# Selective scans on Trainium2: the backward scan written into the PSUM banks of the direction sum, and two fixed pairs of banks

## The chip, the cores and the metric

The kernel runs on one core of one Trainium2 chip. The metric is device time in microseconds, from three runs of the kernel before: 4045.58, 4043.1 and 4032.89 us, median 4043.1. One further execution was profiled.

The engines are named as in the profile: PE is TensorE (PEld its weight loads), DVE is VectorE, ACT is ScalarE, POOL is GpSimd, SP is SyncE. PSUM is the memory into which TensorE writes its sums. [...]

## The reference, cut to what matters

The network has two layers: attention with a mixture of experts, then a state-space layer with another mixture of experts. The change concerns the state-space layer alone. It runs one selective scan in four directions over an image of 32 x 32 positions and averages the four:

```python
def _selective_scan(x, A_log, D, W_delta, b_delta, W_B, W_C):
    delta = jax.nn.softplus(x @ W_delta + b_delta)
    Bm = x @ W_B
    Cm = x @ W_C
    A = -jnp.exp(A_log)
    dA = jnp.exp(delta[..., None] * A)
    dBx = (delta * x)[..., None] * Bm[:, :, None, :]
    ...
    _, h = jax.lax.associative_scan(combine, (dA, dBx), axis=1)
    y = jnp.einsum('blcn,bln->blc', h, Cm) + x * D
    return y
...
out1 = corr(flat)
out2 = jnp.flip(corr(jnp.flip(flat, axis=1)), axis=1)
rows_f = jnp.flip(rows, axis=1).reshape(B, H * W, C)
out3 = jnp.flip(corr(rows_f).reshape(B, H, W, C), axis=1).reshape(B, H * W, C)
cols_f = jnp.flip(cols, axis=1).reshape(B, W * H, C)
out4 = jnp.flip(corr(cols_f).reshape(B, W, H, C), axis=1)
...
mamba_out = (out1 + out2 + out3 + out4) / 4
```

Four images, 256 channels, 16 states and 1024 positions. The state obeys h = dA * h_before + dBx along the direction.

## The kernel before

**Stages.** The attention and the first mixture of experts fill the first 2191 us of the profiled execution, the scans the time from 2191 to 3461, and the second mixture of experts with the output the rest.

**What a scan is.** Channels lie on the 128 partitions, in two channel tiles, positions along the free dimension (1024). A `Scan` is one image, one channel tile and one state: 4 x 2 x 16 = 128 scans, in that order, worked one per *turn*. `turn(k)` gives out the instructions of scan k and of its neighbours in a pipeline, and `tc.manual_schedule()` keeps each engine's instructions in the order in which the code gives them out. So a turn has a fixed order on every engine, and an instruction that waits holds up what stands behind it on its engine.

**The four directions** of scan k become these instructions:

- `decays` (L2025, ScalarE): the decays along rows, into the PSUM tile `da`; a second set along columns (`column_decays`, L2017) and the products of decays along one row (`products`, L2021) lie in SBUF. `inputs` (L2033 GpSimd, L2034 ScalarE) makes the inputs `uu`, in row order and in column order.
- `forth` (L2046, VectorE): the forward scan, into the SBUF tile `h0`. TensorE adds it with the weight `twice` (two times the identity), since two of the four directions start from it.
- `back` (L2055, VectorE): the backward scan over the same decays, read in reverse, into an SBUF tile `h`. TensorE adds it with `ident`.
- `columns` (L2072, VectorE): the scan along columns, into another `h`; TensorE adds it transposed back (L2076).
- `come_in` and `third` (L2061 VectorE, L2066 GpSimd): the direction with flipped rows is the forward state plus a correction, products times a value that comes in for each row. TensorE adds the correction with `ident`.

**The sum.** `add` (L2041) multiplies a view of 1024 states by a weight in two halves of 512, one PSUM bank each, into the two tiles `hp` of the scan. Each of these fp32 matmuls shows as two instructions in the profile, so a direction is a *group* of four. The first group opens the accumulation (`start=True`). `output` (L2082, VectorE) multiplies each half of the sum by C into `yc`, and TensorE adds `yc` over the 16 states into the tile `y` (L2083); after the 16th state `finish` (L2088) adds y to the image. A turn thus has five groups on TensorE: columns and third of scan k-1, forward and backward of scan k, y of scan k-1.

**PSUM in this stage.** [...] The pool of four banks is shared with other steps, which ask it for a bank whenever they need one.

**Other steps in the turns.** At two places of a turn, at its top and after `come_in`, the kernel runs one piece of some other work: `norm` and `route` of the image before (the second mixture of experts' normalisation and routing), `Prep.steps` of the image after (its layer norm, delta, B and C), and `completing`, which fetches and adds results of the first mixture of experts. A piece after `come_in` typically issues TensorE's matmuls, and the piece at the top of the next turn reads them. VectorE reads the means (`nm_mean` L1690, `ln_mean` L1788), the variances (`ln_var` L1800), `ln_rb` (L1819), `raw` (L1703), `sums` (L1631) and `op` (L1911). ScalarE reads `bp` (L1828), `zp` twice (L1851, L1852) and `nm_tp` three times (L1704, L1707). About half of the 128 turns carry such matmuls. TensorE's order in a turn is: columns of k-1, third of k-1, forward and backward of k, y of k-1, then a step's matmuls.

GpSimd has also one indirect DMA in many turns: the routed tokens go out to their slots (L1983), or results are fetched (L1892). SyncE loads B and C of a scan two turns ahead (L2011, L2013).

Of the kernel before, what the change touches and what calls it, by code (L numbers as in the profile page):

```python
# [11 lines left out]
F32 = mybir.dt.float32  # L12
F16 = mybir.dt.float16
BF16 = mybir.dt.bfloat16
# [3 lines left out]
ALU = mybir.AluOpType  # L18
AX = mybir.AxisListType
PSUM = bass.MemoryType.PSUM  # L20

P = 128
# [3 lines left out]
HW = 32  # L26
L = HW * HW
NT = L // P
NTA = B * NT
HALF = 512  # L30
NHALF = L // HALF
# [31 lines left out]
def metaformer(ctx: ExitStack, tc: tile.TileContext, t: dict, out: bass.AP):  # L63
    nc = tc.nc

    cons = ctx.enter_context(tc.tile_pool(name="cons", bufs=1))
    ident = cons.tile([P, P], F32, tag="ident", name="ident")
# [3 lines left out]
    first = cons.tile([P, E], F32, tag="first", name="first")  # L71
# [398 lines left out]
    with ExitStack() as st:  # L470
        wp = st.enter_context(tc.tile_pool(name="a_w", bufs=1))
# [38 lines left out]
        p2 = st.enter_context(tc.tile_pool(name="a_p2", bufs=2))  # L510
# [403 lines left out]
        order = [(b, g, a, n) for b in range(B) for g in range(2) for a in range(NP) for n in range(2)]  # L914
# [13 lines left out]
        for b in range(B):  # L928
            i = b * PER
# [578 lines left out]
    with tc.If(some > 0):  # L1508
# [240 lines left out]
    twice = sw.tile([P, P], F32, tag="twice", name="twice")  # L1749
# [6 lines left out]
    h0s = [sw.tile([P, HW + 2, HW], F32, tag=f"h0_{i}", name=f"h0_{i}") for i in range(2)]  # L1756
    prods = [sw.tile([P, HW + 1, HW], F32, tag=f"prod{i}", name=f"prod{i}") for i in range(2)]
# [4 lines left out]
    def cols_flipped(a):  # L1762
        return a.rearrange("p (r w) -> p w r", w=HW)[:, ::-1, :]

    def grid(a):
        return a.rearrange("p (r w) -> p r w", w=HW)

    class Prep:
# [7 lines left out]
        def steps(self, room, psum, tag):  # L1776
# [62 lines left out]
            def lost(c, cols):  # L1839
                back = self.dx[:, c, cols]  # L1840
                nc.vector.tensor_scalar(back, v[:, c, cols], 1.0, 1.0, ALU.add, ALU.subtract)
                nc.vector.tensor_tensor(back, v[:, c, cols], back, ALU.subtract)
# [146 lines left out]
    with ExitStack() as st:  # L1989
        wp = st.enter_context(tc.tile_pool(name="s_w", bufs=1))  # L1990
        p1 = st.enter_context(tc.tile_pool(name="s_p1", bufs=1))
        p2 = st.enter_context(tc.tile_pool(name="s_p2", bufs=2))
        ps_m = ps_h = st.enter_context(tc.tile_pool(name="s_ps_h", bufs=4, space=PSUM))
        ps_y = st.enter_context(tc.tile_pool(name="s_ps_y", bufs=1, space=PSUM))
        ps_d = st.enter_context(tc.tile_pool(name="s_ps_d", bufs=1, space=PSUM))

        class Scan:

# [2 lines left out]

            def __init__(self, prep, k, c, s):
                self.prep, self.b, self.k, self.c, self.s = prep, prep.b, k, c, s
                self.h0, self.prod = h0s[k % 2], prods[k % 2]
                self.decay = am[:, c, s : s + 1]

            def rows(self):
# [25 lines left out]
                nc.gpsimd.tensor_tensor(self.uu[:, 0], self.prep.dx[:, self.c], self.bb, ALU.mult)  # L2033
                nc.scalar.copy(grid(self.uu[:, 1]), cols_flipped(self.uu[:, 0]))  # L2034

            def add(self, view, eye=None, first=False, last=False):

                if first:
                    self.hp = [ps_h.tile([P, HALF], F32, tag="hp", name="hp") for h in range(NHALF)]
                for h in range(NHALF):  # L2040
                    nc.tensor.matmul(self.hp[h], ident if eye is None else eye, view[:, ts(h, HW // NHALF), :],  # L2041
                                     start=first, stop=last)

            def forth(self):
                rows = self.h0[:, 1 : HW + 1, :]
                nc.vector.tensor_tensor_scan(rows.rearrange("p r w -> p (r w)"), self.da, self.uu[:, 0], 0.0,  # L2046
                                             ALU.mult, ALU.add)
                self.add(rows, eye=twice, first=True)

                self.gap = p2.tile([P, HW], F32, tag="gap", name="gap")  # L2050
                nc.gpsimd.tensor_tensor(self.gap, self.h0[:, 2:, HW - 1], self.h0[:, :HW, HW - 1], ALU.subtract)

            def back(self):
                hs = p2.tile([P, L], F32, tag="h", name="h", bufs=3)
                nc.vector.tensor_tensor_scan(hs[:, ::-1], self.da[:, ::-1], self.uu[:, 0][:, ::-1], 0.0,  # L2055
                                             ALU.mult, ALU.add)
                self.add(grid(hs))

            def come_in(self):
                self.come = p2.tile([P, HW], F32, tag="come", name="come")  # L2060
# [7 lines left out]
                self.add(grid(self.da_c), last=True)  # L2068

            def columns(self):  # L2070
                hs = p2.tile([P, L], F32, tag="h", name="h", bufs=3)
                nc.vector.tensor_tensor_scan(hs, self.da_c, self.uu[:, 1], 0.0, ALU.mult, ALU.add)  # L2072

                half = HW // NHALF
                for h in range(NHALF):
                    nc.tensor.matmul(cols_flipped(self.hp[h]), ident, grid(hs)[:, :, ts(h, half)],  # L2076
                                     start=False, stop=False)

            def output(self, y):
                for h in range(NHALF):  # L2080
                    yc = p2.tile([P, HALF], F32, tag="yc", name="yc", bufs=4)
                    nc.vector.tensor_tensor(yc, self.hp[h], self.cb[:, ts(h, HALF)], ALU.mult)  # L2082
                    nc.tensor.matmul(y[:, ts(h, HALF)], ident, yc, start=(self.s == 0), stop=(self.s == NS - 1))  # L2083

            def finish(self, y):
# [4 lines left out]
        order = [(b, c, s) for b in range(B) for c in range(CT) for s in range(NS)]  # L2090
        scans, steps, ys, cum = [], [], [], None
# [16 lines left out]
        def routed(b):  # L2108
            nonlocal sending
            yield from norm(b, tok, p1, ps_m, "hp", "hp", p1.tile([P, CT, L], F32, tag="xm", name="nm_d"))  # L2110
            yield from route(b, tok, slot, p1.tile([P, NUMBERS], F32, tag="numbers", name="numbers"), ps_m, "hp")
            sending = scatter(b)

        def turn(k):
            nonlocal steps, cum
            if k > 1:
                scans[k - 2].finish(ys[k - 2])
            for step in steps:
                next(step, None)
            next(complete, None)  # L2120
            if 0 <= k + 2 < len(order):
                b, c, s = order[k + 2]
                scans.append(Scan(preps[b], k + 2, c, s))
                scans[k + 2].rows()
            if k == -1:
                scans[0].decays()
            if 0 <= k + 1 < len(order):
                scans[k + 1].column_decays()
            if k > 0:
                scans[k - 1].third()  # L2130
            if 0 <= k + 1 < len(order):
                scans[k + 1].products(cum)
            if 0 <= k < len(order):
                b, c, s = order[k]
                if c == 0 and s == 0:
                    for left in (*steps, sending):
                        assert next(left, "end") == "end"
                    steps = []
                    if b + 1 < B:
                        preps.append(Prep(b + 1))  # L2140
                if b > 0 and c * NS + s == 1:
                    steps.append(routed(b - 1))
                if b + 1 < B and c * NS + s == (BEHIND if b > 0 else 0):
                    steps.append(preps[b + 1].steps(room, ps_m, "hp"))
                ys.append(ps_y.tile([P, L], F32, tag="y", name="y") if s == 0 else ys[-1])
                scans[k].forth()
                scans[k].back()
            if 0 <= k + 1 < len(order):
                if k >= 0:
                    scans[k + 1].decays()  # L2150
                scans[k + 1].inputs()
            next(sending, None)
            if k == NS * CT:
                assert next(complete, "end") == "end"
            if k > 0:
                scans[k - 1].output(ys[k - 1])
            if 0 <= k < len(order):
                scans[k].come_in()
                for step in steps:
                    next(step, None)  # L2160
                next(complete, None)
            if 0 <= k + 2 < len(order) and order[k + 2][2] == 0:

                b, c, _ = order[k + 2]
                if k < 0:
                    cum = lead.cum
                    return
# [17 lines left out]
    with ExitStack() as st:  # L2185
# [71 lines left out]
        with ExitStack() as sa:  # L2257
# [3 lines left out]
            ps_h = sa.enter_context(tc.tile_pool(name="m1_ps_h", bufs=3, space=PSUM))  # L2261
# [132 lines left out]
```

## Time and profile before

| what | value |
|---|---|
| profiled execution, whole | 4047.44 us |
| its span, first to last instruction | 4045.4 us |
| median of the runs | 4043.1 us |
| TensorE busy over the span | 3522.2 us (87%) |
| VectorE busy | 3049.1 us (75%) |
| ScalarE busy | 2818.0 us (70%) |
| GpSimd busy | 1894.3 us (47%) |
| granted TensorE clock over the span | 0.881 |
| each of L2046, L2055, L2072 (scans of 128 x 1024, 127 of the 128) | 2272, 2264, 2274 ns |
| yc, L2082 (128 x 512, 256 times) | 678 ns |
| fp32 matmul of 128 x 512 (L2083) | 592 ns, modelled to its end |

How to read it: the table is over the whole execution, and its stages have different limits, so the busy shares of the scan stage have to be taken by themselves. A matmul's duration contains the drain at its end, which overlaps the next one; how fast a train of matmuls runs is seen from the distance between starts. In a timeline a line has the start, the length, the engine, the source line, the operation, the tiles written and read, the number of instructions merged, and in brackets the idle time of the engine before it with what ended that. In a table of waits a line has who waited for whom, then the sum in us, the number of times and the longest one.

### The profile page before, as it was taken

The numbers are of one execution on the slowest core, as the hardware profiler recorded it, in microseconds if no ns is written. First come the engines' busy times: TensorE is split into PE (matmuls) and PEld (weight loads), VectorE is DVE, ScalarE is ACT, GpSimd is POOL, SyncE is SP. The second block draws the span as 40 slices with busy tenths as digits, with TensorE's granted clock in tenths as the row PEclk, the third lists the DMA queues.
The fourth block names the chain that finished last, engine by engine and source line by source line (L and its number), as shares of the span: only waits on it lengthen the run. The fifth ranks groups of instructions, "written<-read, shape, count | busy, mean of one in ns | idle before, by whom it ended". The sixth has DMA issues, their size and how long they took to land. (4 is left out here: it accounts for less than half of the span.)

```text
span 4045.4 us, 50460 instructions
## 1 busy us (share of the span) xinstructions
PE 3522.2 (87%) x17586; PEld 1963.0 (49%) x17586; DVE 3049.1 (75%) x5439; ACT 2818.0 (70%) x3748; POOL 1894.3 (47%) x1643
## 2 busy tenths in 40 slices
PE   8378888888788878886687999999999999999996
PEld 5134444534354434433564434444444434788885
DVE  2689898988899898987666899899899899411112
ACT  2889999999999998994255666767767677322222
POOL 0145454575548564765453665445445446121111
PEclk8568787788778877788798999999999999999997
DMA  9300093000000000000573333333333334565555
GB/s 293 102 1 1 1 260 90 1 1 30 12 1 1 17 17 1 1 12 22 176 214 120 119 118 122 104 104 125 106 109 122 114 106 135 192 189 188 188 191 188
DMA packets 241818, 393.76 MB, mean 97 GB/s; under 512 B 31888, under 2 KB 182160, under 8 KB 241424
## 3 DMA queue, kind: packets, MB, share of 16 engines
q1 hardware_dynamic: 218016, 340.54, 27.2%
q0 software_dynamic: 19904, 48.48, 3.7%
q8 instruction: 142, 2.33, 0.2%
q10 hardware_dynamic: 3632, 1.40, 0.1%
q14 instruction: 124, 1.02, 0.1%
HBM read 280.41 MB, written 109.94 MB: 96 GB/s over the span
## 5 line engine op out<-in xcount | busy, mean ns | idle before, releaser
L823 POOL TENSOR_SCALAR dr<-s_n,last 128x1024 bf16<-128x1024 f32 x250 | 719.7, 2895 | 734.8 <-DVE state L851 377.2
L733 ACT ACTIVATE junk_a<-s_n,state 128x1024 int8<-128x1024 f32 x448 | 514.6, 1149 | 23.7 <-DVE state L857 7.3
L2066 POOL TENSOR_TENSOR da_c<-prod,come 128x1024 f32<-128x1024 f32 x128 | 248.8, 1944 | 434.6 <-DVE h L2072 383.8
L737 DVE TENSOR_SCALAR_CACHE_REDUCE junk_v<-s_n,state 128x1024 int8<-128x1024 f32 x320 | 408.7, 1277 | 8.8
L2242 ACT ACTIVATE hid<-hp,b 128x256 f32<-128x256 f32 x288 | 133.7, 474 | 355.7 <-PE hp L2240 355.5
L784 DVE SCALAR_TENSOR_TENSOR w<-s_n,win 128x1024 f32<-128x1024 f32 x256 | 350.4, 1369 | 5.3
L787 DVE MAX8 win<-w 128x8 f32<-128x1024 f32 x256 | 314.5, 1228 | 8.8
L891 ACT ACTIVATE ex<-sT 128x1024 f32<-128x1024 f32 x256 | 247.1, 1016 | 88.7 <-PE sT L883 88.7
L2033 POOL TENSOR_TENSOR uu<-dx,bb 128x1024 f32<-128x1024 f32 x127 | 302.9, 2385 | 1.5 <-DMA bb<-bc_d 1.4
L733 ACT ACTIVATE junk_a<-s_n,guess 128x1024 int8<-128x1024 f32 x256 | 294.3, 1149 | 7.2
L2072 DVE TENSOR_TENSOR_SCAN h<-da_c,uu 128x1024 f32<-128x1024 f32 x127 | 288.8, 2274 | 0.0
L2046 DVE TENSOR_TENSOR_SCAN h<-da,uu 128x1024 f32<-128x1024 f32 x127 | 288.5, 2272 | 0.0
L2055 DVE TENSOR_TENSOR_SCAN h<-da,uu 128x1024 f32<-128x1024 f32 x127 | 287.5, 2264 | 0.0
L901 PE MATMUL o_ps<-ex,vT 128*32 128x256 f32 x2048 | 239.0, 451 | 54.0 <-ACT ex L891 42.2
L2017 ACT ACTIVATE da_c<-delta,a_log 128x1024 f32<-128x1024 f32 x128 | 268.5, 2097 | 5.3 <-DMA rows_y<-ys 5.2
L2076 PE MATMUL hp<-h,ident 128*128 128x512 f32 x512 | 248.9, 609 | 21.8 <-DVE h L2072 21.6
L2240 PE MATMUL hp<-xe,w 128*128 128x256 f32 x1152 | 258.6, 381 | 6.6 <-DVE xe L2228 6.4
L2251 DVE TENSOR_TENSOR ys<-yp,b2e 128x512 f32<-128x512 f32 x36 | 24.9, 692 | 317.2 <-PE yp L2248 305.1
L2253 POOL DMA_INDIRECT results<-ys,to x72 | 69.9, 970 | 409.2 <-DVE ys L2251 185.2
L767 ACT COPY s_n<-sp 128x1024 f32<-128x1024 f32 x256 | 245.3, 1003 | 19.1 <-PE sp L759 11.5
L2248 PE MATMUL yp<-w2e,hid 128*128 128x256 f32 x1152 | 255.9, 379 | 0.0
L2034 ACT COPY uu<-uu 128x1024 f32<-128x1024 f32 x127 | 252.3, 1987 | 2.5 <-POOL uu L2033 2.5
(646 smaller groups left out, 7787.0 us busy)
## 6 DMA issues: line engine op xcount, KB each, us to landing
cb<-bc_d SPq DMA_DIRECT2D x128, 512.0 KB, 4.0
bb<-bc_d SPq DMA_DIRECT2D x127, 512.0 KB, 4.9
w<-in_w SPq DMA_DIRECT2D x36, 1024.0 KB, 5.0
w2e<-in_w SPq DMA_DIRECT2D x36, 1024.0 KB, 5.6
slots_x<-zeros SPq DMA_DIRECT2D x1, 33669.0 KB
slots_x<-zeros SPq DMA_DIRECT2D x1, 33282.0 KB
w<-in_w SPq DMA_DIRECT2D x72, 256.0 KB, 3.1
xs<-slots_x SPq DMA_DIRECT2D x36, 261.0 KB, 3.8
```

Of the source, the lines that this page charges most:

```text
L733: nc.scalar.activation(junk, self.row(r), AF.Sign, bias=thr, scale=-1.0, accum_out=u)
L737: nc.vector.tensor_scalar(junk, self.row(r), thr, None, ALU.is_lt, ALU.add, accum_out=u)
L784: nc.vector.scalar_tensor_tensor(w, self.row(r), self.win[:, r, 0:1], self.row(r), ALU.is_gt if r < LAST_DVE else ALU.is_ge, ALU.subtract, ...
L787: nc.vector.max(out=self.win[:, r, 1:], in_=w)
L823: ins = eng.tensor_scalar(dr, self.row(r), self.last[:, r : r + 1], None, ALU.is_lt)
L2017: nc.scalar.activation(grid(self.da_c), cols_flipped(self.prep.delta[:, self.c]), AF.Exp, scale=self.decay)
L2033: nc.gpsimd.tensor_tensor(self.uu[:, 0], self.prep.dx[:, self.c], self.bb, ALU.mult)
L2046: nc.vector.tensor_tensor_scan(rows.rearrange("p r w -> p (r w)"), self.da, self.uu[:, 0], 0.0, ALU.mult, ALU.add)
L2055: nc.vector.tensor_tensor_scan(hs[:, ::-1], self.da[:, ::-1], self.uu[:, 0][:, ::-1], 0.0, ALU.mult, ALU.add)
L2072: nc.vector.tensor_tensor_scan(hs, self.da_c, self.uu[:, 1], 0.0, ALU.mult, ALU.add)
L2240: nc.tensor.matmul(hp[:, f % 2], self.w1[:, c, ts(f, P)], self.xe[:, c], start=(c == 0), stop=(c == CT - 1))
L2248: nc.tensor.matmul(yp[:, a], self.hid[:, f, ts(a, P)], self.w2[:, f, :], start=(f == 0), stop=(f == NF - 1))
```

## The change

The backward scan is no longer written to SBUF and added by TensorE. VectorE writes it straight into the two PSUM banks in which the scan's directions are summed, and TensorE adds the others onto it. [...] So before the scan, `begin` writes zeros with two bf16 matmuls of 512 columns (`nought`, one per bank) that open the accumulation. The forward states are then added after the backward scan, in `back`.

The four rotating banks become two fixed tiles `sum0` and `sum1` of two banks each; scan k owns `sums[k % 2]`. Other steps no longer ask a pool: `Spare` gives them the two halves of the pair that is not scan k's, from the output of scan k-1 (`ps_m.open(k)` stands after `come_in`) until `begin` of scan k+1 in the next turn. `begin` stands after the step pieces at the turn's top, and the matmuls of the column direction, before given out with the scan at a turn's end, stand behind it. TensorE's order in a turn becomes: opening pair of k, columns of k-1, third of k-1, forward addition of k, y of k-1, a step's matmuls. The column states `h` have two buffers instead of three (one such tile per turn instead of two).

```diff
-        ps_m = ps_h = st.enter_context(tc.tile_pool(name="s_ps_h", bufs=4, space=PSUM))
+        ps_h = st.enter_context(tc.tile_pool(name="s_ps_h", bufs=1, space=PSUM))
...
+        sums = [ps_h.tile([P, L], F32, tag=f"sum{i}", name=f"sum{i}") for i in range(2)]
+        nought = wp.tile([P, P], BF16, tag="nought", name="nought")
+        nc.vector.memset(nought, 0.0)
+
+        class Spare:
+
+            def open(self, k):
+                self.left = [sums[(k + 1) % 2][:, ts(h, HALF)] for h in range(NHALF)]
+
+            def tile(self, shape, dt, tag, name):
+                part = self.left.pop(0)
+                return part.rearrange("p (i c) -> p i c", c=shape[2]) if len(shape) == 3 else part
+
+        ps_m = Spare()
...
-            def add(self, view, eye=None, first=False, last=False):
-
-                if first:
-                    self.hp = [ps_h.tile([P, HALF], F32, tag="hp", name="hp") for h in range(NHALF)]
+            def begin(self):
+
                 for h in range(NHALF):
-                    nc.tensor.matmul(self.hp[h], ident if eye is None else eye, view[:, ts(h, HW // NHALF), :],
-                                     start=first, stop=last)
+                    nc.tensor.matmul(self.sum[:, ts(h, HALF)], nought, nought[:, 0:1].to_broadcast([P, HALF]),
+                                     start=True, stop=False)
+
+            def add(self, view, eye=None, last=False):
+
+                for h in range(NHALF):
+                    nc.tensor.matmul(self.sum[:, ts(h, HALF)], ident if eye is None else eye,
+                                     view[:, ts(h, HW // NHALF), :], start=False, stop=last)
...
-                self.add(rows, eye=twice, first=True)
...
             def back(self):
-                hs = p2.tile([P, L], F32, tag="h", name="h", bufs=3)
-                nc.vector.tensor_tensor_scan(hs[:, ::-1], self.da[:, ::-1], self.uu[:, 0][:, ::-1], 0.0,
+                nc.vector.tensor_tensor_scan(self.sum[:, ::-1], self.da[:, ::-1], self.uu[:, 0][:, ::-1], 0.0,
                                              ALU.mult, ALU.add)
-                self.add(grid(hs))
+                self.add(self.h0[:, 1 : HW + 1, :], eye=twice)
...
             def columns(self):
-                hs = p2.tile([P, L], F32, tag="h", name="h", bufs=3)
-                nc.vector.tensor_tensor_scan(hs, self.da_c, self.uu[:, 1], 0.0, ALU.mult, ALU.add)
-
+                self.hs = p2.tile([P, L], F32, tag="h", name="h")
+                nc.vector.tensor_tensor_scan(self.hs, self.da_c, self.uu[:, 1], 0.0, ALU.mult, ALU.add)
+
+            def columns_added(self):
                 half = HW // NHALF
                 for h in range(NHALF):
-                    nc.tensor.matmul(cols_flipped(self.hp[h]), ident, grid(hs)[:, :, ts(h, half)],
+                    nc.tensor.matmul(cols_flipped(self.sum[:, ts(h, HALF)]), ident, grid(self.hs)[:, :, ts(h, half)],
                                      start=False, stop=False)
...
             next(complete, None)
+            if 0 <= k < len(order):
+                scans[k].begin()
+            if k > 0:
+                scans[k - 1].columns_added()
...
                 scans[k].come_in()
+                ps_m.open(k)
                 for step in steps:
```

In `output` the two halves of `self.sum` take the place of the two tiles `self.hp`.

More of the change, by code (lines that the diff above doesn't have):

```diff
@@ L2003, in __init__ @@
                 self.prep, self.b, self.k, self.c, self.s = prep, prep.b, k, c, s
-                self.h0, self.prod = h0s[k % 2], prods[k % 2]
+                self.h0, self.prod, self.sum = h0s[k % 2], prods[k % 2], sums[k % 2]
                 self.decay = am[:, c, s : s + 1]
@@ L2081, in output @@
                     yc = p2.tile([P, HALF], F32, tag="yc", name="yc", bufs=4)
-                    nc.vector.tensor_tensor(yc, self.hp[h], self.cb[:, ts(h, HALF)], ALU.mult)
+                    nc.vector.tensor_tensor(yc, self.sum[:, ts(h, HALF)], self.cb[:, ts(h, HALF)], ALU.mult)
                     nc.tensor.matmul(y[:, ts(h, HALF)], ident, yc, start=(self.s == 0), stop=(self.s == NS - 1))
```

## The prediction

> **What bounds the kernel now.** I read the busy time by stage first. The scan stage is the only one the diff touches, and two engines are nearly full in it: TensorE works 1227 of its 1270 us, VectorE 1147 (span start to end, length, then busy time and instructions per engine, granted clock, DMA).
>
> ```profile
> 2191.00:3461.00 1270.00, 1227.35 (x3013) 533.99 (x3014) 1147.36 (x1123) 874.67 (x681) 673.94 (x464) 0.99 0.36 115
> ```
>
> So a TensorE saving can give at most what VectorE idles there, 1270 - 1147 = 123 us. VectorE's waits say how much of that is TensorE's load and how much is plain latency:
>
> ```profile
> DVE yc L2082 <- PE hp L2041: 28.7, 63, 2.4
> DVE lg L1703 <- PE raw L1701: 20.8, 12, 1.8
> DVE x L2088 <- PE y L2083: 14.4, 8, 2.1
> DVE nm_d L1690 <- PE nm_mean L1687: 12.1, 6, 2.0
> DVE xm L1788 <- PE ln_mean L1785: 11.1, 6, 3.7
> ```
>
> Then the timeline, turn by turn, from one L2046 to the next. A turn without extra steps late in the stage:
>
> ```profile
> 3392.63 2.27 DVE L2046 TENSOR_TENSOR_SCAN h<-da,uu 128x1024 f32<-128x1024 f32 x1
> 3394.82 2.27 DVE L2055 TENSOR_TENSOR_SCAN h<-da,uu 128x1024 f32<-128x1024 f32 x1
> 3397.44 0.69 DVE L2082 TENSOR_TENSOR yc<-hp,cb 128x512 f32<-128x512 f32 x1 [0.36 <-PE hp L2041]
> ...
> 3394.66 1.88 PE L2076 MATMUL hp<-h,ident 128*128 128x512 f32 x4
> 3396.38 1.88 PE L2041 MATMUL hp<-da_c,ident 128*128 128x512 f32 x4
> 3398.10 1.88 PE L2041 MATMUL hp<-h,twice 128*128 128x512 f32 x4
> ```
>
> Scans start 2.18 us apart, groups of four matmuls 1.72 us apart. TensorE has five groups a turn, 5 x 1.72 = 8.58, which is this turn's length; VectorE alone needs 7.86 (the turn from 3334.00 to 3341.85 has no idle). Elsewhere extra steps (norms, routing, preparing the next batch) stretch VectorE to 9 to 12 us, or put a sixth group on TensorE (10.30).
>
> **The change, part by part.** Removed: one group a turn, the backward addition, 1.72 us of TensorE. Added: two bf16 matmuls of 512 columns. A bf16 matmul with 128 columns takes 0.057 us of a train (16 in 1.07 us; less the last one's own 0.22, 15 distances), so four times as many columns 0.23, the pair 0.46, and with a restart after a wait 0.5. The other bound is the fp32 spacing, 0.43 each, 0.96. I take 0.5, as bf16 is the nearer row:
>
> ```profile
> 219.80 1.07 PE L883 MATMUL sT<-drop,dr 128*128 128x128 bf16 x16
> ```
>
> A plain turn then needs 4 x 1.72 + 0.5 = 7.4 of TensorE: VectorE becomes the bound, at 7.86. The forward addition now waits for the backward scan, and that is covered: y ends 0.2 us into a turn, the opening pair 0.7, columns 2.4, third 4.15 (yc needs its second half at 4.97), the backward scan 4.45, and the addition starts at 4.6, when the backward one did. Without that cover it would cost up to 1.72.
>
> Moved: the column additions go behind the opening pair and behind the steps' readers. This is the new wait. The pair for scan k+1 uses the banks in which the steps of turn k left their sums, so it waits until VectorE or ScalarE has read these; behind it on TensorE stand columns, third and the next addition, and VectorE's backward scan waits for the pair itself; behind that scan stand yc, come and columns, and ScalarE's L2025, which reuses the decays' banks and had 1.15 us of idle to spare in plain turns. Before, the columns' group ran during that reading. Memset, DMA issues and the queues of SyncE and GpSimd have nothing moved past them (one memset, before the stage's first turn).
>
> Scan into PSUM: no row has it. Reading from PSUM costs nothing visible (L2046, from PSUM, 2272 ns; L2072, from SBUF, 2274), ScalarE writes PSUM in 1115 ns (L2025) and SBUF in 1146 (L2021). That bounds it at -0.03 us below; above, by the farthest row, a whole further pass at 1.225 us (L2088). I take 0, nearest to the first pair, since only the memory differs there. [...]
>
> By kind of turn:
> - Plain turns bound by TensorE (116 to 127 of 0 to 127, 8.58 each): 12 x (8.58 - 7.86) = 8.7; turns 23, 24, 30 (0.59, 0.67, 0.73): 2.0. Gain 10.7.
> - Turns in which VectorE waits for y at a channel tile's end (L2088). y is now there at 4.6 + 2 x 1.72 + 0.2 = 8.24 into a turn, VectorE arrives at 7.85: 0.4 idle instead of 2.15 (three times), 1.43, and 1.1 in turn 16. Gain 5.2 + 1.0 + 0.7 = 6.9.
> - Steps read by VectorE (means, variances, raw). Most of their idle stays: the path is backward scan, addition, y, step, read, and the addition has only changed its name. Turns 33, 34: 11.18 now and after. What goes is backlog: turn 1 (12.82 to 11.18), 25 (idle 3.1 to the 0.7 of turn 26), 40 and 72 (12.31 to 11.18), five with 0.4 to 1.0: 1.6 + 2.4 + 2.3 + 2.7 = 9.0.
> - Steps read by ScalarE lose. From the zp group's start to the end of ScalarE's second reading are 2715.23 - 2712.04 = 3.19; then 0.1, the pair 0.5, and four groups 6.88: 10.67 a turn against 10.30. With the two bp turns before them, in which the pair waits for one reading of 0.58 and holds the backward scan by 1.3 and 0 us, and 2.0 before the first zp turn, turns 47 to 53 come to 8.5 + 11.5 + 8.2 + 11.7 + 3 x 10.67 = 71.9 against 69.5: batch 1 loses 2.4, batch 2 (70.8 before) 1.1, batch 0, where results are added in the same turns, gains 1.0. The four nm_tp turns of three batches (ScalarE reads until 1.1 us into the next turn) lose 0.7 a batch. Loss 2.4 + 1.1 - 1.0 + 2.1 = 4.6.
>
> ```profile
> 2712.04 1.88 PE L1847 MATMUL zp<-xm,wd 128*128 128x512 f32 x4
> ...
> 2714.55 0.68 ACT L1852 ACTIVATE sp<-zp,bd 128x512 f32<-128x512 f32 x1
> ```
>
> - Turn 0: its backward scan stood 3.1 us for a DMA that reads the buffer it overwrites; in PSUM it need not, but column decays wait for the same DMA. [...]
> - Clock. TensorE idles more, in stretches of over 2 us in some ten turns of 10 to 12.5 us. Before, a window of 3.4 us that was busy 1.04 or 1.40 us was followed by one at half clock, one busy 1.68 was not:
>
> ```profile
> 2987.10:2990.50 3.40, 1.04 (x10) 0.85 (x8) 3.40 (x3) 1.48 (x1) 0.00 (x0) 1.00 0.52 192
> 2990.50:2993.90 3.40, 3.40 (x4) 1.49 (x5) 3.40 (x4) 1.15 (x1) 1.92 (x2) 0.51 0.00 0
> 3301.20:3304.60 3.40, 1.40 (x4) 0.68 (x4) 3.40 (x2) 0.09 (x1) 1.31 (x1) 1.00 0.13 53
> ...
> 2669.70:2673.10 3.40, 1.68 (x4) 0.68 (x4) 3.40 (x4) 0.00 (x0) 1.59 (x1) 1.00 0.05 19
> ```
>
> Half a clock over 3.4 us is 1.7 us of TensorE, of which the next turn's slack (about 0.5) hides part: 1.2. I take three more such windows that matter, a loss of 3. [...]
>
> Sum: 10.7 + 6.9 + 9.0 - 4.6 + 1 - 3 = 20 us. The end gains nothing more: the last yc waits for the last scatter's DMA (5.1 us idle), which moves with turn 127. The profiled execution took 4047.4 (span 4045.4 and 2 around it), so 4027; the shown runs' median, 4043.1, lies 4 below it, so 4023.
>
> **The rivals.**
> - The opening is dear (0.96 instead of 0.5). For: it follows a wait every time and switches weights. Against: the bf16 row. Some 24 turns (12 zp, 12 nm_tp) run around TensorE and pay 0.46: 11 less, 4034, no change that can be measured (within 0.3%, 12 us, which is about what runs of this kernel tell apart).
> - The clock. For: the half windows above, and VectorE will be the bound in most turns. Against: in plain turns TensorE stays 94% loaded. If each of the 65 turns that carry a step's matmuls were followed by a half window, 65 x 1.2 = 78 less 20: 4101. It decides from 17 such turns (20 / 1.2); 27 of them give 4055, slower.
> - The scan into PSUM is slower. For: it would read and write PSUM at once, which no row shows. Against: a scan takes 2.1 ns an element, and ScalarE writes 1024 of them into PSUM in 1115 ns, half of that. It cancels the gain from 20 / 128 = 0.16 us a scan; at 0.25 the time is 4055, at the upper bound of 1.225 it is 4180.
> - The waits that I let go are latency too. For: most of VectorE's 115 us of waiting is the unchanged path above. Against: turns of the same kind without backlog (26, 33) are shorter. Without the 9.0 and 6.9 the gain is 4, the time 4039: no measurable change.
>
> **How the numbers follow.** Forecast 0.58: faster, 4006 to 4031. The dear opening 0.12 and waits that stay 0.10, together 0.22: 4032 to 4054. Clock 0.10, scan into PSUM 0.10: slower, from 4055. The best end: scan 4 faster, no clock loss (3), turn 0 (4), a low run (6): 4023 - 17 = 4006. The upper end takes in the whole second case and stops at 4054, where the slow cases begin, with 2 in 10 left out. Chances: faster by over 0.3% 0.58, within 0.22, slower 0.20.
>
> **What would show it.** In the changed profile: the backward additions (two groups' worth of x512) gone; pairs of bf16 matmuls of 0.2 us; turns 116 to 127 at 7.86; yc idle near 0; in zp turns the backward scan idle for the opening pair, turns of 10.7; L2055's successor still at 2.27 us; fewer than ten windows at half clock. I am wrong if that scan is over 2.4 us, if the pair takes nearly 1 us, or if backward scans wait in plain turns.

## The result, and the profile after

| | before | changed |
|---|---|---|
| median of 12 runs each, us | 4044.06 | 4048.23 |
| lowest to highest, us | 4032.89 to 4052.62 | 4032.59 to 4052.15 |
| ratio to before, 95% interval | | 1.000, 0.9985 to 1.0015 |
| profiled execution (its span), us | 4047.4 (4045.4) | 4032.7 (4030.7) |
| start of the first forward scan, us | 2191.29 | 2176.40 |
| scan stage: first to last forward scan, us | 1252.85 | 1252.85 |
| from the last forward scan to the end of the span, us | 601.3 | 601.5 |

The forecast was 20 us faster; nothing was gained. The two profiled spans differ by 14.7 us, but all of that lies ahead of the first forward scan (2191.29 - 2176.40 = 14.9), where the diff adds no more than one memset. So from here on kernels are compared by their scan stage, from the start of turn 0's forward scan to that of turn 127: 1252.85 us in both.

The stage in the changed kernel, busy time by engine (columns as in the prediction's window: PE, PEld, DVE, ACT, POOL, each with its instructions, granted clock, DMA share, GB/s):

```profile
2176.00:3446.00 1270.00, 1096.51 (x2758) 464.88 (x2757) 1147.66 (x1123) 874.90 (x681) 669.26 (x464) 0.98 0.36 115
```

TensorE lost 131 us of work (1227 to 1097). VectorE works as long as before (1147.4, now 1147.7) in as long a stretch. So its idle time, which was to shrink, is the same 122 us, and only its place has moved. VectorE's waits in that stretch:

```profile
DVE yc L2100 <- PE sum L2060: 46.7, 37, 2.8
DVE lg L1703 <- PE sum L1701: 13.6, 12, 1.5
DVE nm_d L1690 <- PE sum L1687: 12.1, 6, 2.0
DVE sum L2072 <- PE sum L2054: 11.5, 26, 1.3
```

The output product yc waits 46.7 us instead of 28.7, in 37 places instead of 63: the many small waits of the plain turns have gone and fewer, longer ones have come. The wait of the backward scan L2072 for the opening pair L2054 is new. Where the opening pair itself waits (TensorE's waits, same stretch):

```profile
PE sum L2054 <- ACT sum L1707: 22.8, 12, 1.9
PE sum L2054 <- ACT sp L1852: 13.5, 10, 1.4
PE sum L2054 <- DVE xm L1819: 13.0, 5, 3.5
PE sum L2054 <- DVE x L1911: 12.0, 8, 2.1
```

A plain turn, which starts at 3350.66 and ends at 3358.51 (timeline):

```profile
3350.66 2.27 DVE L2065 TENSOR_TENSOR_SCAN h<-da,uu 128x1024 f32<-128x1024 f32 x1
3350.84 0.60 PE L2054 MATMUL sum<-nought 128*128 128x512 bf16 x2
3351.28 1.88 PE L2094 MATMUL sum<-h,ident 128*128 128x512 f32 x4
3352.84 2.27 DVE L2072 TENSOR_TENSOR_SCAN sum<-da,uu 128x1024 f32<-128x1024 f32 x1
3352.99 1.88 PE L2060 MATMUL sum<-da_c,ident 128*128 128x512 f32 x4
3355.02 1.27 DVE L2100 TENSOR_TENSOR yc<-sum,cb 128x512 f32<-128x512 f32 x2
```

No line of VectorE has idle time in brackets, and the turn takes 7.86 us instead of 8.58. The opening pair costs 0.44 (3350.84 to 3351.28). So the first part of the forecast came true; the loss is elsewhere. Turn 37, one of the turns in which a norm's sums are read by ScalarE (nm_tp), before:

```profile
2566.83 1.96 PE L2076 MATMUL hp<-h,ident 128*128 128x512 f32 x4
2567.11 2.28 DVE L2046 TENSOR_TENSOR_SCAN h<-da,uu 128x1024 f32<-128x1024 f32 x1
...
2568.63 1.88 PE L2041 MATMUL hp<-da_c,ident 128*128 128x512 f32 x4
```

and in the changed kernel:

```profile
2551.05 0.17 DVE L1703 COPY lg<-sum 128x16 f32<-128x16 f32 x1 [1.01 <-PE sum L1701]
2551.14 2.28 DVE L2065 TENSOR_TENSOR_SCAN h<-da,uu 128x1024 f32<-128x1024 f32 x1
2551.26 0.59 ACT L1704 COPY tok<-sum 128x512 f32<-128x512 f32 x1 [2.82 <-DVE lg L1703]
...
2552.91 0.59 PE L2054 MATMUL sum<-nought 128*128 128x512 bf16 x2 [1.89 <-ACT sum L1707]
2553.34 1.88 PE L2094 MATMUL sum<-h,ident 128*128 128x512 f32 x4
2553.59 2.30 DVE L2072 TENSOR_TENSOR_SCAN sum<-da,uu 128x1024 f32<-128x1024 f32 x1 [0.17 <-PE sum L2054]
...
2555.05 1.88 PE L2060 MATMUL sum<-da_c,ident 128*128 128x512 f32 x4
...
2556.97 1.29 DVE L2100 TENSOR_TENSOR yc<-sum,cb 128x512 f32<-128x512 f32 x2 [1.08 <-PE sum L2060]
```

Before, the columns started 0.28 us ahead of the turn, beside ScalarE's reading, and the third group 1.52 us into it. Now the order is: ScalarE has read (1.71 into the turn), opening pair (1.77), columns (2.20), third (3.91), and yc at 5.83, 1.08 us after VectorE was free for it. The turn takes 10.54 us instead of 9.87.

Two differences stand in these lines, and either could be the cause. The **order**: columns and third stand behind the opening pair, and that behind the readers. The **whole pair as one tile**: ScalarE's tok waits for VectorE's lg, though they read different halves, and yc's first half starts after all four matmuls of the third group and not after its own two. A third difference is the **clock**: ten stretches at half clock (granted clock 0.5; each lasts 3.4 us, two of them 6.8) lie in the stage, against three before.

### The profile page after: what moved, and what is told of

Read it like the earlier page. It is cut to its first block, busy times and chain, and to the rows that moved or that the text cites. A ratio compares the mean times of both kernels' runs of the same rounds, so it can differ in the third digit from the quotient of the medians.

```text
span 4030.7 us, 49782 instructions
## 1 busy us (share of the span) xinstructions
PE 3380.4 (84%) x17330; PEld 1890.6 (47%) x17330; DVE 3050.2 (76%) x5440; ACT 2816.5 (70%) x3748; POOL 1887.5 (47%) x1643
## 5 line engine op out<-in xcount | busy, mean ns | idle before, releaser
L2083 POOL TENSOR_TENSOR da_c<-prod,come 128x1024 f32<-128x1024 f32 x128 | 247.0, 1930 | 466.3 <-DVE h L2089 442.2
L2072 DVE TENSOR_TENSOR_SCAN sum<-da,uu 128x1024 f32<-128x1024 f32 x127 | 289.3, 2278 | 11.5 <-PE sum L2054 11.5
L2065 DVE TENSOR_TENSOR_SCAN h<-da,uu 128x1024 f32<-128x1024 f32 x127 | 288.6, 2272 | 1.0 <-POOL uu L2048 1.0
L2094 PE MATMUL sum<-h,ident 128*128 128x512 f32 x512 | 256.9, 626 | 35.5 <-DVE h L2089 35.5
L2060 PE MATMUL sum<-h,twice 128*128 128x512 f32 x512 | 251.9, 615 | 41.4 <-DVE sum L2072 41.4
L767 ACT COPY s_n<-sp 128x1024 f32<-128x1024 f32 x256 | 245.4, 1003 | 25.4 <-PE sp L759 17.8
```

Of the source, the lines that this page charges most:

```text
L2072: nc.vector.tensor_tensor_scan(self.sum[:, ::-1], self.da[:, ::-1], self.uu[:, 0][:, ::-1], 0.0, ALU.mult, ALU.add)
```

## The experiments

Where no ratio is given, the scan stage of one profiled execution is what is compared. Half-clock stretches do not fall alike in two executions of one kernel: e5 and e8 below are the same kernel and have nearly the same stage, yet turns 1, 12 and 111 differ by 1.7, 1.7 and 2.5 us between them. So what a kernel does is read from the turns at full clock, and a few us of a stage mean little.

**e1: columns first.** The two calls in `turn` exchanged:

```diff
-            if 0 <= k < len(order):
-                scans[k].begin()
             if k > 0:
                 scans[k - 1].columns_added()
+            if 0 <= k < len(order):
+                scans[k].begin()
```

> One edit to the changed kernel: in each turn the column matmuls of the turn before are issued ahead of the opening pair instead of behind it. Measure: the scan stage, from the start of the first forward scan to the start of the last, 1252.85 us in the kernel before and in the changed one. Theory A (order: the opening pair stands behind the readers of the side steps, the column matmuls stand behind the opening pair, and so the first output product of the turn comes late): the opening pair's 87 us of waits no longer hold the columns, the 46.7 us that the output product (yc) waits for TensorE falls towards the 28.7 us of before, and the stage falls to about 1235 us. Theory B (both banks of a pair are one tile, so a reader of the first half waits for the matmuls of the second): nothing of that is touched, stage 1249 to 1256, turn 36 still 10.5. Theory C (half-clock windows): stage moves only with the number of such windows, about 1.5 us for each of the nine.

Measured: stage 1278.07 us, 25 longer; execution 4071.2. The expected 1235 was missed, but turn by turn the reason shows. 25 turns are shorter, by 22.8 together: turns 36 to 38 at 9.82 instead of 10.54, 50 to 53 (zp) about 0.57 shorter each; 4.6 of it is half clock that turns 13, 69 and 102 have in the changed kernel and not here. Turn 37 there:

```profile
2574.83 1.96 PE L2094 MATMUL sum<-h,ident 128*128 128x512 f32 x4
...
2575.11 2.28 DVE L2065 TENSOR_TENSOR_SCAN h<-da,uu 128x1024 f32<-128x1024 f32 x1
...
2576.87 0.59 PE L2054 MATMUL sum<-nought 128*128 128x512 bf16 x2
2577.30 1.88 PE L2060 MATMUL sum<-da_c,ident 128*128 128x512 f32 x4
...
2579.77 1.27 DVE L2100 TENSOR_TENSOR yc<-sum,cb 128x512 f32<-128x512 f32 x2
```

The opening pair still comes 1.76 into the turn, but the columns are done by then, and yc starts at 4.66 with no idle time. In 50 other turns the edit costs 0.44 us each, 22.0 together: where no reader holds the opening pair, it used to run while TensorE waited for the column states, and now it stands between columns and third. That is also the price of the opening pair on the path. In 16 turns it costs 0.6 to 2.7, 25.4 together, most of it half clock (17 stretches). Turn 42 of this kernel shows how:

```profile
2626.51 1.88 PE L2060 MATMUL sum<-da_c,ident 128*128 128x512 f32 x4
...
2630.29 3.30 PE L2060 MATMUL sum<-h,twice 128*128 128x512 f32 x4 [1.90 <-DVE sum L2072]
```

Columns, opening pair and third are done earlier, so TensorE then waits 1.90 us in one piece for the backward scan (in the changed kernel 1.38 ahead of the opening pair and 0.37 here); a half-clock stretch begins at 2630.81, and the forward addition takes 3.30 us instead of 1.88. The turn is 1.69 longer than in the changed kernel (11.72 against 10.03).

**e2: one tile per bank.** The call of a scan names one output tile, so the backward scan becomes two, and the upper half of its states goes through SBUF:

```diff
+        sums = [[ps_h.tile([P, HALF], F32, tag=f"sum{i}{h}", name=f"sum{i}{h}") for h in range(NHALF)]
+                for i in range(2)]
...
+                for h, states in ((1, upper), (0, self.sum[0])):
+                    nc.vector.tensor_tensor_scan(states[:, ::-1], self.da[:, ts(h, HALF)][:, ::-1],
+                                                 self.uu[:, 0, ts(h, HALF)][:, ::-1], start, ALU.mult, ALU.add)
+                    start = upper[:, 0:1]
+                self.add(self.h0[:, 1 : HW + 1, :], eye=twice)
+                nc.tensor.matmul(self.sum[1], ident, upper, start=False, stop=False)
```

> The changed kernel with each pair as two tiles of one bank each. One scan can't write two tiles, so the backward scan is two scans of 512, the second starting from the last state of the first; only the lower half goes into PSUM, the upper one through SBUF and one more matmul group of half the size (TensorE: +0.94 us and one opening matmul of 0.22 less, so plain turns stay at VectorE's 7.86 plus what a second scan instruction costs, 0 to 0.2 us, 0 to 25 us over the stage). Theory B (whole-pair tracking): output products and readers wait for their own half again, the first yc of turn 36 comes about 0.9 earlier, yc's waits for TensorE fall from 46.7 to below 30 us, ScalarE's token copy no longer waits for VectorE's logit copy; stage 1252.9 - 20 + the price of the second scan, 1233 to 1258, with the mean of turns 36 to 38 at 10.0 or below. Theory A (order): step turns unchanged, stage 1253 to 1278. Theory C: as theory A.

Measured: stage 1312.85; a miss above every range. The second scan cost 0.32 us a turn (plain turns 8.18), 41 over the stage, more than the 0.2 that I had allowed, and the additional half group lengthens turns that TensorE sets. So the stage decides nothing, but the places do. Turn 37 (it starts at 2576.64):

```profile
2576.20 0.59 ACT L1704 COPY tok<-sum 128x512 f32<-128x512 f32 x1 [2.40 <-PE sum L1699]
...
2577.85 0.38 PE L2054 MATMUL sum<-nought 128*128 128x512 bf16 x1 [1.34 <-ACT sum L1707]
2578.06 1.88 PE L2099 MATMUL sum<-h,ident 128*128 128x512 f32 x4
...
2579.78 1.88 PE L2060 MATMUL sum<-da_c,ident 128*128 128x512 f32 x4
...
2581.34 1.27 DVE L2105 TENSOR_TENSOR yc<-sum,cb 128x512 f32<-128x512 f32 x2
```

tok waits for its own transposes and starts 0.44 ahead of the turn, the opening comes at 1.21 instead of 1.77, and yc at 4.70 without idle time, while the third group (3.14 to 5.02) still runs. So with the order unchanged, one tile per bank also removes yc's wait, and TensorE's idle time ahead of the opening falls from 1.89 to 1.34. The turn's length hides it, 10.72, since the half group makes TensorE's work 9.38 in it instead of 8.65; 8.65 + 1.34 = 9.99 is my estimate without that, against 10.54 in the changed kernel and 9.87 before. Turn 39, where TensorE doesn't set the length, shows it: 8.27, before's 7.94 and the 0.32 of the second scan, instead of 9.43. Since either edit takes most of these turns' loss away, the loss needs both: the order and the common tile.

**e3: both edits.**

> Both edits together: tiles of one bank each, and the column matmuls ahead of the opening. If A and B are separate losses the gains add: stage about 1215 to 1240. If one alone is the cause, this equals the better of the two within 4 us. If neither (theory C, half-clock windows), stage at or above 1253.

Measured: stage 1308.82, 4 us from e2. In the nm_tp turns the gains don't add: at full clock they are 10.72 and, the fourth, 8.27 in both. Only zp turns went further (9.66, against 9.96 in e1 and 11.17 in e2), while 16 half-clock stretches, against 8 in e2, took much of it back.

**e4: fixed pairs alone.** Backward states through SBUF as before, the forward states open the banks:

```diff
+                self.add(rows, eye=twice, first=True)
...
+                hs = p2.tile([P, L], F32, tag="h", name="h", bufs=3)
+                nc.vector.tensor_tensor_scan(hs[:, ::-1], self.da[:, ::-1], self.uu[:, 0][:, ::-1], 0.0,
+                                             ALU.mult, ALU.add)
+                self.add(grid(hs))
...
                 scans[k].columns()
+                scans[k].columns_added()
```

> The fixed pairs alone: the side steps still share the two pairs, but the backward states go through SBUF and a fourth matmul group as before, the forward states open the banks (no opening pair), and the columns are issued at the end of their turn. It tells the two parts of the change apart. If the loss lies in the fixed shared pairs (A or B), the stage is longer than before's 1252.9: plain turns 8.58 as before and step turns as in the changed kernel, 1265 to 1275. If the loss lies with the scan into PSUM and its opening pair, the stage is 1250 to 1256, as before.

Measured: stage 1262.08, between the two ranges. The turns tell more: 36 to 39, 51 to 53 and 83 to 85 have before's lengths to 0.01 us (9.87, 7.94, 10.30), and the plain ones are 8.58 again. ScalarE's tok waits for lg here too, and it costs nothing, as the columns stand ahead of it:

```profile
2567.70 1.96 PE L2096 MATMUL sum<-h,ident 128*128 128x512 f32 x4
...
2568.09 0.59 ACT L1704 COPY tok<-sum 128x512 f32<-128x512 f32 x1 [2.33 <-DVE lg L1703]
```

The 9.2 us over before's stage are 2.0 in turn 1 (half clock), 0.4 to 0.7 each in ten others, 1.3 each in 12 and 112, less 0.9 in 0 and 25. In turn 23, one of the ten, yc waits 1.03 us for the third group, where it waited 0.18 and 0.17 before. So the fixed pairs alone cost the norm's turns nothing: their loss comes only with the opening pair ahead of the columns. Elsewhere the pairs cost several us by themselves.

**e5: the order by reader.** Columns first only where the last steps in the pair were nm_tp, bp or zp, the ones that ScalarE reads:

```diff
+                self.slow = self.slow or name in ("nm_tp", "bp", "zp")
...
+            if ps_m.slow and k > 0:
+                scans[k - 1].columns_added()
             if 0 <= k < len(order):
                 scans[k].begin()
-            if k > 0:
+            if k > 0 and not ps_m.slow:
                 scans[k - 1].columns_added()
```

> The changed kernel with the column matmuls ahead of the opening pair only in turns whose pair was last used by the side steps that ScalarE reads (the transposes with their raw logits, the B/C rows and the softplus inputs: nm_tp, bp, zp); in all others the opening pair stays first. With columns first in every turn the turns of those steps fell (36 to 38: 10.54 to 9.82 us each, 50 to 53: 10.53 to 9.96, sum of all that fell -22.8 us), 50 others rose by 0.44 us, which is the opening pair itself put between columns and third group (+22.0), and 16 rose by 0.6 to 2.7 (+25.4), most of them by a window of half clock. Theory A (order): the falls stay and the 0.44 goes, stage 1252.9 - 20 = about 1233 us (1229 to 1240). If the half clock is tied to the order in those turns too: 1240 to 1252. Theory B (whole-pair tracking) gives no gain from order at all: 1253.

Measured: stage 1235.03, execution 4034.0. The order theory had 1233. Turns 36 to 39 are 9.82, 9.82, 9.82, 8.23, zp turns 9.96, plain turns 7.86.

**e6 and e7: TensorE kept busy with zeros**, eight bf16 matmuls into the output bank, in e6 behind the third group of those turns of e5 in which the columns go first, in e7 ahead of the opening pair of the changed kernel. The edit of e7:

```diff
+            if k > 0 and len(ps_m.left) < NHALF:
+                scans[k - 1].warm(ys[k - 1], 8)
             if 0 <= k < len(order):
                 scans[k].begin()
```

> As the kernel with the order chosen by reader, and in those same turns eight more matmuls of zeros (bf16, 128 x 512, about 1.7 us together, added to the output bank y, so they add nothing to the sums) behind the third group, where TensorE then waits for the backward scan. Theory C (windows of half clock come from TensorE's idle stretches and cost up to 1.7 us each): fewer windows in those turns, and a stage 2 to 8 us shorter than without the zeros. If half clock costs nothing there, or the zeros come late enough to push the forward matmuls back, the stage is equal or up to 10 us longer.

> The changed kernel in its own order, with eight matmuls of zeros into the output bank y ahead of the opening pair in each turn whose pair the side steps used, where TensorE waits for the readers (gaps of 1.5 to 3.7 us in front of the opening pair). It measures what the half-clock windows cost the changed kernel (10 in its scan stage, against 3 in the kernel before). Theory C: windows 10 -> 4 or fewer, turns 69 and 102 fall from 12.24 to 10.54, stage 1252.9 -> 1242 to 1248. Theory A alone: windows may fall, but the stage moves by less than 4 us, since turns 36 to 39 and 50 to 53 still have their waits; where the gap is shorter than 1.7 us the zeros add to it, up to +15 us.

Measured: e6 1255.29, 20 worse than e5, with nine half-clock stretches against eight: the zeros pushed the forward addition back (36: 10.57). e7 1259.11, with the stretches down from ten to five. Turns 69 and 102 fell from 12.24 to 10.54, as expected, and 12, 13 and 15 by 1.07, 1.26 and 1.26; together some 7 us that half clock costs the changed kernel. But the zeros cost 0.2 to 1.2 us in turns whose gap was shorter, such as 4, 44 and 51. Half clock is a real loss and not the main one.

**e8: e5 again, timed.**

> The kernel with the order chosen by reader again, now timed in rounds against the kernel before. Its scan stage was 17.8 us shorter (1235.03 against 1252.85), and nothing outside the stage was touched. If the stage is all that differs, the median is 0.44% below that of the kernel before: ratio 0.9956, about 4026 us beside 4044, with the interval below 1. If the half-clock windows that such a kernel draws vary from run to run by as much as the gain, the interval holds 1.

Measured: 4025.64 us (median of 6, 4016.33 to 4029.15) beside 4048.22 (median of 11); ratio 0.9947, interval 0.9932 to 0.9961; stage 1234.82. It is faster than both kernels, by half a per cent; the changed one was not timed beside it, but its lowest run (4032.59) lies above all six.

**e9 and e10: who reads the pair first.** ScalarE's copy given out ahead of VectorE's, in the changed kernel (e9) and in e5 (e10):

```diff
-            nc.vector.tensor_copy(lg1[:, ts(r, 2)], raw)
             nc.scalar.copy(tok[:, ts(r, 2), :C], tp)
+            nc.vector.tensor_copy(lg1[:, ts(r, 2)], raw)
```

> The changed kernel with two lines of norm() exchanged: ScalarE's token copy (tok, L1704) is given out ahead of VectorE's copy of the logits (lg, L1703). Both read the pair, in different halves. In the changed kernel tok starts 0.12 us into turn 37, behind lg; in the kernel before, and with one tile per bank, 0.44 us ahead of the turn. Theory B (waits follow the whole pair, in the order in which the program gives the instructions out): tok starts 0.44 ahead, the squares behind it end 0.5 earlier, the opening pair comes at 1.2 to 1.3 instead of 1.77, turns 36 to 38 fall from 10.54 to about 10.0, and the stage by 5 to 8 us, 1252.9 to about 1246 (plus or minus 4 for half-clock windows). Without theory B (tok waits for lg for another reason, or their order is set elsewhere): tok stays at 0.12, stage as it was.

> The kernel with the order chosen by reader, with the same two lines exchanged. The columns no longer stand behind the opening pair in these turns, so its 0.5 us earlier end frees only the backward scan (which started 2.45 us into the turn instead of 2.20): at most 0.25 us in 12 turns, 3 us of the stage, 1235 to 1232 us. Ratio to the kernel before about 0.994 as without the exchange (0.9947), within its interval. If the exchange holds VectorE's logits back instead, these turns grow by up to 0.6 us and the stage by 7.

Measured: e9 1252.20; e10 1240.05, ratio 0.9962 (0.9949 to 0.9975), no better than e8. Turn 37 of e9 starts at 2564.90 (L1703 and L1704 have changed places):

```profile
2564.19 0.59 ACT L1703 COPY tok<-sum 128x512 f32<-128x512 f32 x1 [2.29 <-PE sum L1701]
2564.81 0.17 DVE L1704 COPY lg<-sum 128x16 f32<-128x16 f32 x1 [1.63 <-ACT tok L1703]
2564.90 2.28 DVE L2065 TENSOR_TENSOR_SCAN h<-da,uu 128x1024 f32<-128x1024 f32 x1
...
2566.05 0.38 PE L2054 MATMUL sum<-nought 128*128 128x512 bf16 x1 [1.90 <-ACT sum L1707]
```

The opening pair comes at 1.15, a little earlier than expected, and yet turns 36 and 38 keep their 10.54 (37 itself has half clock): tok waits for raw, which lies in the other half, lg waits for tok, and the forward scan stands behind lg. TensorE is idle for 1.90 us ahead of the opening pair, as in the changed kernel (1.89). Turn 39 is 0.6 shorter and turn 35 0.6 longer. The readers of one pair go one after the other whichever comes first. The exchange moved the wait to VectorE.

## Why the prediction was wrong

The stage's change by kind of turn, from the distances between forward scans (us; the predicted clock loss of 3 was not laid on any turns, and turn 127 has no next scan):

| turns | predicted | changed | order by reader (e8) |
|---|---|---|---|
| plain, 116 to 126 | -8.0 (11 of the 12) | -8.0 | -8.0 |
| 23, 24, 30 | -2.0 | +0.3 | +0.3 |
| channel tile's end (16, 32, 64, 96, 112) | -6.9 | -7.3 | -7.3 |
| read by VectorE (1, 25, 40, 72; 3, 43, 75, 108, taken for four of the five that the prediction doesn't name) | -9.0 | -7.1 | -5.4 |
| nm_tp, 36 to 39, 68 to 71, 100 to 103 | +2.1 | +13.9 | +0.4 |
| bp and zp, batches 1 and 2 (47 to 53, 79 to 85) | +3.5 | +4.6 | +0.3 |
| batch 0, turns 8 to 15, 17, 18 | -1.0 | +5.9 | +3.9 |
| turn 0 | -1 | -1.6 | -1.6 |
| 111 and all others | 0 | -0.6 | -0.6 |
| sum | -22.3; with turn 127 (-0.7) and clock (+3) -20 | 0.0 | -18.0 |

**The step that failed** is the sentence "The four nm_tp turns of three batches (ScalarE reads until 1.1 us into the next turn) lose 0.7 a batch", with the batch 0 term beside it. The mechanism was named: the pair waits for ScalarE, and columns and third stand behind it. Its size was not: 2.1 against 13.9. I had worked it with the waits of the trace before, where each bank was a tile of its own. There ScalarE's copy started 0.44 ahead of turn 37 and its last reading ended 1.16 into it:

```profile
2566.67 0.59 ACT L1704 COPY tok<-nm_tp 128x512 f32<-128x512 f32 x1 [1.90 <-PE nm_tp L1699]
...
2568.07 0.20 ACT L1707 ACTIVATION_READ_ACCUMULATOR nm_tp<-nm_tp 128x1 f32 x1
```

With the pair as one tile the copy begins after lg, and the last reading ends at 1.71:

```profile
2552.66 0.19 ACT L1707 ACTIVATION_READ_ACCUMULATOR sum<-sum 128x1 f32 x1
```

The first three turns of a batch are TensorE's: 8.65 us of work and the 1.89 ahead of the opening pair make 10.54. With a tile per bank those 1.89 were 1.34 (e2), so 0.55 of the 0.67 lost in such a turn is ScalarE's later start. The wait of yc isn't on their path, for VectorE waits another 1.01 for raw at their end. It is in the fourth turn, which is VectorE's: there yc waits 1.08, because its first half waits for the whole third group, 0.86 (two spacings of 0.43) longer than for its own two matmuls, and the backward scan waits 0.17. That turn loses 1.5. Together this is 10.5; half clock in turns 69 and 102 adds 2 x 1.69.

**Second, backlog that stayed**: turns 1, 23 and 24. I had 1.6 less for turn 1; it lost 0.07. Turns 23 and 24 became 8.99 from 8.45 and 8.53, where I had 7.86. I had read 23 and 24 as bound by TensorE's load. But their third group waits for GpSimd's product (`third`, L2066 before, L2083 now), and it still does. Turn 23 before (it starts at 2433.77) and in the changed kernel (2421.22):

```profile
2437.22 1.99 PE L2041 MATMUL hp<-da_c,ident 128*128 128x512 f32 x4 [0.34 <-POOL da_c L2066]
2438.39 0.69 DVE L2082 TENSOR_TENSOR yc<-hp,cb 128x512 f32<-128x512 f32 x1 [0.18 <-PE hp L2041]
```

```profile
2424.67 1.98 PE L2060 MATMUL sum<-da_c,ident 128*128 128x512 f32 x4 [0.96 <-POOL da_c L2083]
2426.69 1.29 DVE L2100 TENSOR_TENSOR yc<-sum,cb 128x512 f32<-128x512 f32 x2 [1.02 <-PE sum L2060]
```

Third starts 3.45 into the turn in both, and yc now waits for all of it. With a tile per bank these turns take 8.46 and 8.39, although the second scan costs 0.32 in them (e2), and with the pairs alone 8.99 and 9.00 (e4). So it is the common tile again. In turn 1 third waits 1.33 for the same product and yc 1.92 for third.

**Third, batch 0**, where returned results (op) and zp share the turns: +5.9 where I had -1.0. About 3.6 of it is half clock (12, 13, 15, by e7); the rest lies in readers in the same pair: in turn 8 (10.43 instead of 8.77) the opening pair waits for ScalarE's reading of bp until 2.85 into the turn, the backward scan 1.28 for the opening pair and yc 1.07 for third, and in turns 11 and 12 VectorE's reading of op waits 2.2 for ScalarE's of zp. e8 keeps +3.9 there, 1.7 of it half clock in turn 12; what makes up the rest stays open.

**Right**: the bound of plain turns, the price of the opening pair (0.5 forecast, 0.43 to 0.44 measured; no run adds to a bank that no matmul had opened), the channel tiles' ends, zp turns (10.67 forecast, 10.53 measured), and the scan into PSUM at nothing (2278 ns against 2264 in SBUF: 14 ns measured, 28 in e1, with 2292). No run shows the term of 1 us for turn 0 as I set it; there the backward scan waits for no DMA any more (3.07 us before), the column decays still do (5.15 us, before 5.16), and the turn is 1.6 us shorter. Two terms were added loosely, without consequence: three windows at 1.2 are 3.6 and not 3, and the dear opening's 0.96 comes out only with a restart of 0.1 on top of two spacings of 0.43.

**The rivals.** The dear opening fell with the 0.44. The dear scan fell with 2278 ns. Half clock after each of 65 turns fell: ten stretches, of which about 7 us matter, twice my 3. "Waits that stay" came nearest, with 4039 and no measurable change, but for the wrong reason: most waits that I let go did go (ends of channel tiles, 25, 40, 72), and others took their place. A gain of the size that I forecast was there to be had by the order of two calls: with the order by reader the stage is 18 us shorter, against a forecast of 20. That the two numbers lie so close is luck: by the table, e8 falls short by 3.6 in the turns read by VectorE, 2.3 in 23, 24 and 30 and 4.9 in batch 0, and the turns read by ScalarE make up 4.9 of it, since their columns no longer stand behind the opening pair.

## What to carry to other kernels

When an operation that opens a buffer is put into an in-order engine's queue, look for its latest reader in each kind of turn, and at what is queued behind it that goes to another buffer: that work should stand ahead of the opening where the reader is late (turns 36 to 38 took 9.82 us so and 10.54 the other way), and behind it where the opening then runs in an idle moment (the other way cost 0.44 us in each of 50 turns of e1). When two buffers become one tile, take every wait of the old trace anew, since readers and writers of its halves waited for each other here: tok started 0.12 us into turn 37 instead of 0.44 ahead of it. A stage in which one engine lost 131 us of work and another idles as long as before has only moved its waits; turn lengths by kind show where to.

## What the runs showed of the hardware

Work that is done earlier can cost clock. In e1 the same groups ran earlier in turn 42, TensorE's idle time came in one piece of 1.90 us instead of two of 1.38 and 0.37, and the next group ran at half clock, 3.30 us instead of 1.88; the kernel had 17 such stretches against ten. The windows around turn 69 of the changed kernel (columns as above):

```profile
2872.70:2876.10 3.40, 1.51 (x9) 1.06 (x8) 2.79 (x3) 2.69 (x6) 2.02 (x3) 1.00 0.42 172
2876.10:2879.50 3.40, 3.40 (x5) 1.33 (x4) 1.88 (x1) 3.33 (x4) 2.07 (x1) 0.52 0.00 0
```

A window in which TensorE was busy for 1.51 of 3.40 us, 44%, is followed by one at 0.52. The busy share alone doesn't tell which windows are: in e2 a window (2585.90 to 2589.31) that shows 2.07 of 3.41 us busy, in matmuls of 8, 128 and 512 columns, was followed by one at 0.50, while before one of 1.68 (2669.70 to 2673.10) was followed by one at 1.00.

Splitting a scan is dear: two of 512 columns (1198 ns into SBUF, 1292 ns into PSUM from a stored state) lengthen a turn by 0.32 us against one of 1024 in 2278 ns.
